# Stores of folded attention weights moved behind the first spreads of B, dt and C, with one fold kept in the scan's tiles

## The chip, the cores and the metric

The kernel runs on one core of a Trainium2 chip. The metric is the device time of one execution in microseconds (us), the median of three runs. A profile was taken of one further execution; its times count from the start of its span. TensorE, VectorE, ScalarE and GpSimd stand in the profile as PE, DVE, ACT and POOL, the queue from which most transfers are issued as SP. A "q" behind an engine's name means its instruction queue.

## The reference, cut to what matters

The input x is an image of 2 x 128 x 64 x 64 (batch, channels, height, width), in float32. Four layers follow each other. Layer 0 is a small Mamba network with two blocks over the 4096 pixels as a sequence; layer 1 is attention over all pixels whose q, k and v come from 3x3 convolutions; layer 2 is the same kind of attention with 1x1 convolutions; layer 3 fuses four scales. The change lies in layer 0 and in the preparation of layer 1's convolution weights:

```python
dbl = u @ xproj_w.T
dt, Bm, Cm = jnp.split(dbl, [R, R + N], axis=-1)
dt = jax.nn.softplus(dt @ dt_w.T + dt_b)
dA = jnp.exp(dt[..., None] * A)
dBu = (dt * u)[..., None] * Bm[:, :, None, :]

def step(h, inp):
    dA_t, dBu_t, C_t = inp
    h = dA_t * h + dBu_t
    y = jnp.einsum('bdn,bn->bd', h, C_t)
```

Here the inner width is 256, there are 16 states per channel, and u is the activated result of a short convolution. In layer 1:

```python
q = conv2d(x, Wq, bq, 1).reshape(b, c, n)
k = conv2d(x, Wk, bk, 1).reshape(b, c, n)
v = conv2d(x, Wv, bv, 1).reshape(b, c, n)
```

## The kernel before, in words

**Items, groups and slots.** Layer 0 is cut into 32 items: 2 images, 2 blocks, 8 pieces of 512 tokens. Each item has 8 groups of 32 channels. A group's tile h is 128 x 4 x 512: its partitions are 4 sets of states by 32 channels, and 4 states per set lie behind one another. So a group takes one product on VectorE that makes dBu (`times_b`, L389), four decays on ScalarE that make dA (`decay`, L396), four scans on VectorE (`scan`, L407), the product with C on GpSimd (L410), and matmuls that sum over the states (`y_pair`, L422).

A slot is one scan; an item has 32 slots, numbered 0 to 31, and a group has four. The order of all instructions is written out by hand: for every item i and every slot the function `slot` issues the group's own work, and then what `background(i)` has put on that slot's list with `at(slot, function, ...)`. Each engine, and the SP queue, takes its instructions in this order. The background of item i prepares item i + 1 and finishes items i - 1 and i - 2. Items -2 and -1 have no scans; their slots prepare item 0.

**What scans need.** The small projection of an item is in the tile dbl (`xproj_out`, L343, slot 14). `spread_bc` stores its B and C part to a DRAM tile dr (L349, only with B) and loads it back four times with a broadcast over 32 partitions each (L354): B into the tile bb in slot 14, C into the tile cb in slot 22. `spread_dt` copies a group's 32 rows of dt four times, into the four quarters of the tile dtb (L378); `slot` calls it for group g + 3 at the beginning of group g, so the dt of group 0 stands in slot 20 of item -1, that of group 1 in slot 24, of group 2 in slot 28, and of group 3 in slot 0 of item 0. The first product of item 0 stands in slot 26 of item -1, its first decay in slot 28, its first scan in slot 0 of item 0.

**The folds.** Layer 1's 3x3 convolutions are computed from weights combined beforehand. In item -1, `load_rest` (slot 1) issues the loads of three raw weight tiles and of the second image. `fold(k)` for k = 0, 1, 2 (slots 8, 9, 10) makes two tiles ulo and uhi of 128 x 9 x 128 from raw k with ten VectorE instructions (L195 to L204), and stores each to a DRAM tile ufold (L206). They are loaded again (L604, L858) after the scans, about 2096 us into the span.

**Buffers.** The raw weights, the folds' results, the convolution weights cw, the scan's h and the hidden tile of the feed-forward part share one ring of five buffers, tag "h". bb and cb have two buffers each. A new tile takes the buffer that was released first, and its first writer waits for the last user of that buffer. Eight semaphores serve the transfers in turn.

Of the kernel before, what the change touches and what calls it, by code (L numbers as in the profile page):

```python
# [6 lines left out]
F32 = mybir.dt.float32  # L7
# [6 lines left out]
B, C, H, W = 2, 128, 64, 64  # L14
N = H * W
P = 128
# [51 lines left out]
def tile_conv_seq(ctx: ExitStack, tc, x, consts, vecs, wemb, wlay, wconv, wdt, wqkv, wsmall, wms, out):  # L68
# [47 lines left out]
    with tc.manual_schedule(), ExitStack() as s:  # L116
# [4 lines left out]
        sp = scans.enter_context(tc.tile_pool(name="l0s", bufs=1, side="right"))  # L121
# [48 lines left out]
                nc.vector.tensor_tensor(u[:, k, :], cw[:, KC, :], cw[:, k, :], ALU.mult)  # L170
            wu.append(u), am.append(a)

        raws = []

        def load_rest():
            for which in range(3):
# [13 lines left out]
        def fold(which):  # L190

            g = [raws[which][:, :, k, :] for k in range(3)]
            lo, hi = (sp.tile([P, 3, 3, C], F32, name=n, tag="h", bufs=5) for n in ("ulo", "uhi"))
            tt, ts, stt = nc.vector.tensor_tensor, nc.vector.tensor_scalar, nc.vector.scalar_tensor_tensor
            tt(lo[:, 1], g[0], g[2], ALU.add)  # L195
            ts(lo[:, 1], lo[:, 1], -1.0 / 6, None, ALU.mult)
            stt(lo[:, 0], g[1], 1.0 / 6, lo[:, 1], ALU.mult, ALU.add)
            stt(lo[:, 1], g[1], -1.0 / 6, lo[:, 1], ALU.mult, ALU.add)
            stt(hi[:, 0], g[2], 4.0, g[0], ALU.mult, ALU.add)
            ts(hi[:, 0], hi[:, 0], 1.0 / 24, None, ALU.mult)  # L200
            stt(lo[:, 2], g[1], -1.0 / 12, hi[:, 0], ALU.mult, ALU.add)
            stt(hi[:, 0], g[1], 1.0 / 12, hi[:, 0], ALU.mult, ALU.add)
            ts(hi[:, 1], g[0], 0.25, None, ALU.mult)
            nc.vector.tensor_copy(hi[:, 2], g[2])  # L204
            for k, u in enumerate((lo, hi)):
                nc.sync.dma_start(ufold[which][:, 9 * k : 9 * k + 9, :], u.rearrange("p s y c -> p (s y) c"))  # L206


# [9 lines left out]
        def has(i):  # L218
            return 0 <= i < NI
# [269 lines left out]
        def background(i):  # L489

            todo = [[] for _ in range(NSL)]

            def at(t, f, *a):
                todo[t].append((f, a))

            n, p, q, r = i + 1, i - 1, i - 2, i + 2
            if has(q):
                at(3, gelu, q)
                at(6, ffn_down, q, (0, 1)), at(7, ffn_down, q, (2, 3)), at(9, ffn_add, q)
                at(11, out_mm, q), at(12, out_add, q)  # L500
            if has(p):
                at(7, y_out, p, 1), at(7, gate, p)
                at(9, mix_out, p), at(11, mix_add, p)
            if has(n):
                at(0, pu_taps, n, 0, (0, 1)), at(1, pu_taps, n, 0, (2, 3)), at(2, pu_out, n, 0)
                at(3, pu_taps, n, 1, (0, 1)), at(4, pu_taps, n, 1, (2, 3)), at(5, pu_out, n, 1)
                at(13, xproj, n), at(14, xproj_out, n), at(14, spread_bc, n, 0), at(22, spread_bc, n, 1)
                at(15, dtproj, n, 0), at(16, dtproj, n, 1), at(17, soft_plus, n), at(18, dt_end, n)
            if has(i):
                at(1, pz_mm, i, 0), at(3, pz_out, i, 0)  # L510
                at(5, pz_mm, i, 1), at(6, pz_out, i, 1)
            if has(i) or has(n):
                at(11, silu, i, n)
            if i == -1:
                at(1, load_rest), at(7, prepare, 1)
                for k in range(3):
                    at(8 + k, fold, k)
                at(19, spread_dtu, 0), at(26, times_b, 0)
            pair = [(k, second) for k, second in ((p, True), (r, False)) if has(k)]
            if has(r):  # L520
                at(10, embed, r), at(11, embed_out, r)
            w, m = {}, len(pair)
            for k, (it, second) in enumerate(pair):
                at(12 + 2 * k, ln_centre, w, k, it)
                at(13 + 2 * k, ln_square, w, k, it)
                at(27, ln_spread, w, k, m), at(28, ln_scale, w, k, it)
                at(29, ln_shift, w, k, it, second)
            if pair:
                at(17, ln_var, w, m), at(18, ln_eps, w, m), at(19, ln_rs, w, m), at(20, ln_newton, w, m), at(21, ln_step, w, m)
            if has(p):  # L530
                for f in range(4):
                    at(30 + f // 2, ffn_up, p, f)
            if has(i):
                at(24, y_out, i, 0)
            return todo
# [23 lines left out]
        for i in range(-2, NI):  # L559
            todo = background(i)  # L560
            for t_ in range(NSL):
                slot(i, todo, t_)
        todo = background(NI)
        for t_ in range(8):
            slot(NI, todo, t_)
# [321 lines left out]
        for k in range(8, 2 * NSL):  # L887
            if k == NSL:
                todo = background(NI + 1)
            for _ in range(int(beside[k - 8]) if k - 8 < len(beside) else 0):  # L890
                next(steps, None)
            slot(NI + k // NSL, todo, k % NSL)
# [4 lines left out]
        sp = s.enter_context(tc.tile_pool(name="ats", bufs=1, reuse_waits="tile"))  # L897
        psa = s.enter_context(tc.tile_pool(name="atpa", bufs=2, reuse_waits="tile", space=PSUM))
        psm = s.enter_context(tc.tile_pool(name="atpm", bufs=1, reuse_waits="tile", space=PSUM))
        for now in range(NALL + LAG + 10):  # L900
            r, u = divmod(now, NU)
# [71 lines left out]
    with ExitStack() as s, tc.manual_schedule():  # L973
        sp = s.enter_context(tc.tile_pool(name="mss", bufs=1, reuse_waits="tile"))
# [494 lines left out]
```

## Time and profile before

| what | value |
|---|---|
| median of three runs | 5001.07 us (5000.54 to 5005.86) |
| the profiled execution, its time | 5004.69 us |
| the profiled execution, its span | 5002.9 us |
| PE busy | 4661.3 us, 93% of the span |
| DVE busy | 4024.6 us, 80% |
| ACT busy | 2358.8 us, 47% |
| POOL busy | 2337.5 us, 47% |
| scans (L407), 1024 of them | 1241.6 us, 1.27 us each |
| products with B (L389), 256 of them | 581.7 us, 2.27 us each |
| decays (L396), 1024 of them | 681.5 us, 0.68 us each |

The scans of layer 0 run from 73 to some 2090 us, the two attentions and layer 3 follow. A row of the timeline has the start in us, the duration in us, the engine, the line of the kernel, the operation, the tile written and the tiles read, the shapes, how many such instructions were merged, and in brackets how long the engine was idle before and what ended that. For SP the duration of a row is the time in which its transfers were issued, not the time that they took. In a DMA view the stretch is cut into 40 equal parts; one line gives the busy share of the 16 DMA engines in tenths, another the rate in GB/s.

### The profile page before, as it was taken

How to read it: one execution, taken by the hardware profiler on the slowest of the kernel's cores; microseconds unless marked ns; L12 is line 12 of the kernel's file. 1: busy time of each engine (PE TensorE's matmuls, PEld its weight loads, DVE VectorE, ACT ScalarE, POOL GpSimd, SP SyncE). 2: the span in 40 equal slices, each digit the busy share in tenths (PEclk: the TensorE clock that was granted, in tenths of full speed). 3: DMA queues.
4: the chain of work that ended last, by engine and by line, in shares of the span. 5: the costliest groups of instructions: out<-in, count | busy, mean ns of one | idle time of the engine just before them, and what ended most of it. 6: DMA issues, size and time to landing. Idle time of an engine off the chain costs nothing. (4 is left out here: it accounts for less than half of the span.)

```text
span 5002.9 us, 48954 instructions
## 1 busy us (share of the span) xinstructions
PE 4661.3 (93%) x14797; PEld 2242.4 (45%) x14797; DVE 4024.6 (80%) x4283; ACT 2358.8 (47%) x3218; POOL 2337.5 (47%) x1974
## 2 busy tenths in 40 slices
PE   5889999999988899899999999999999999999997
PEld 1222222222222222366667766666666666333332
DVE  6999999999999999878886677767776775667776
ACT  4677777777777777522222222233333332323332
POOL 3777776766777777513332133333333332333331
PEclk8898889989999989899999999999999999999998
DMA  6333333322323333214444344434443443000000
GB/s 163 69 68 68 69 71 70 69 65 62 72 67 68 70 73 73 73 53 113 109 110 123 105 112 111 120 95 114 110 100 98 112 113 88 3 7 7 5 7 9
DMA packets 242343, 386.24 MB, mean 77 GB/s; under 512 B 88592, under 2 KB 88992, under 8 KB 233632
## 3 DMA queue, kind: packets, MB, share of 16 engines
q1 hardware_dynamic: 192928, 315.94, 26.0%
q10 hardware_dynamic: 49152, 67.17, 5.4%
q8 instruction: 118, 1.93, 0.2%
q14 instruction: 145, 1.19, 0.1%
HBM read 101.02 MB, written 13.37 MB: 23 GB/s over the span
## 5 line engine op out<-in xcount | busy, mean ns | idle before, releaser
L792 POOL COPY pt<-tr 32x512 f32<-32x512 f32 x1024 | 650.8, 636 | 1437.3 <-DVE tr L785 704.7
L407 DVE TENSOR_TENSOR_SCAN h<-da,carry,h 128x512 f32<-128x512 f32 x1024 | 1241.6, 1266 | 59.7 <-ACT da L396 30.7
L410 POOL TENSOR_TENSOR h<-h,cb 128x2048 f32<-128x2048 f32 x256 | 1160.9, 4535 | 21.0 <-POOL carry L409 0.4
L755 PE MATMUL pq<-k,q 128*128 128x512 f32 x2048 | 962.6, 593 | 7.0 <-DVE sc L760 7.0
L805 PE MATMUL po<-pt,vt 128*128 128x256 f32 x4096 | 965.7, 379 | 2.5 <-DMA pt<-tr 2.5
L770 ACT ACTIVATE sc<-sc,nm 128x2048 f32<-128x2048 f32 x256 | 510.6, 1995 | 912.8 <-DVE nm L766 701.6
L805 PEld LDWEIGHTS po<-pt,vt 128*128 128x128 f32 x4096 | 777.9, 190 | 294.8 <-issue 208.3
L760 DVE TENSOR_SCALAR_CACHE_REDUCE sc<-pq 128x1024 f32<-128x1024 f32 x512 | 625.1, 1222 | 315.6 <-PE pq L755 294.3
L396 ACT ACTIVATE da<-dtb,am 128x512 f32<-128x512 f32 x1024 | 681.5, 684 | 230.5 <-DVE h L407 207.9
L389 DVE TENSOR_TENSOR h<-bb,pdu 128x2048 f32<-128x2048 f32 x256 | 581.7, 2272 | 86.0 <-PE py L422 29.3
L785 DVE STREAM_TRANSPOSE tr<-sc 128x2048 f32<-128x2048 f32 x256 | 591.6, 2311 | 64.6 <-DMA pt<-tr 56.2
L422 PE MATMUL py<-h,sel 128*32 128x512 f32 x2048 | 511.0, 643 | 1.6 <-POOL h L410 1.6
L755 PEld LDWEIGHTS pq<-k,q 128*128 128x128 f32 x2048 | 382.9, 190 | 283.2 <-issue 247.2
L383 PE MATMUL pdu<-dtu,fsel 128*128 128x512 f32 x512 | 325.3, 721 | 117.0 <-DVE h L389 114.8
L422 PEld LDWEIGHTS py<-h,sel 128*32 128x32 f32 x2048 | 115.2, 117 | 415.0 <-issue 409.5
L310 PE MATMUL pu<-xn,wu 128*128 128x512 f32 x512 | 246.2, 614 | 2.6 <-ACT xn L300 1.7
L383 PEld LDWEIGHTS pdu<-dtu,fsel 128*128 128x128 f32 x512 | 95.9, 214 | 322.0 <-DVE h L389 199.5
L409 POOL COPY carry<-h 128x4 f32<-128x4 f32 x256 | 47.8, 187 | 394.5 <-DVE h L407 392.7
L1219 DVE TENSOR_TENSOR ov<-v,pw 128x2048 f32<-128x2048 f32 x64 | 146.2, 2285 | 62.1 <-PE pw L1212 62.1
L1153 PE MATMUL pqkv<-f,ws 128*128 128x512 f32 x384 | 188.2, 615 | 3.0 <-DVE prod L1170 2.3
L1223 POOL TENSOR_TENSOR ov<-ov 128x2048 f32<-128x2048 f32 x16 | 72.6, 4538 | 235.5 <-DVE ov L1219 235.5
L370 POOL TENSOR_TENSOR dtu<-dt,u 128x1024 f32<-128x1024 f32 x32 | 75.1, 2348 | 192.6 <-ACT dt L364 192.6
(259 smaller groups left out, 5266.6 us busy)
## 6 DMA issues: line engine op xcount, KB each, us to landing
pt<-tr SPq DMA_DIRECT2D x2048, 64.0 KB, 2.0
dtb<-dt SPq DMA_DIRECT2D x1024, 64.0 KB, 2.0
pt<-tr ACTq DMA_DIRECT2D x1024, 64.0 KB, 2.2
bb<-dr SPq DMA_DIRECT2D x128, 256.0 KB, 4.4
cb<-dr SPq DMA_DIRECT2D x128, 256.0 KB, 4.6
uw<-ufold SPq DMA_DIRECT2D x12, 576.0 KB, 4.3
uw<-dkept SPq DMA_DIRECT2D x20, 288.0 KB, 3.0
xt<-in_x SPq DMA_DIRECT2D x16, 256.0 KB, 4.6
```

The costliest lines, as they stand in the source:

```text
L383: nc.tensor.matmul(pdu, lhsT=four(s_ % 4), rhs=st[i]["dtu"][:, s_ // 4, :], start=True, stop=True)
L389: nc.vector.tensor_tensor(h, st[i]["bc", 0], pdu.unsqueeze(1).to_broadcast([P, 4, CH]), ALU.mult)
L396: nc.scalar.activation(da, st[i]["dtb", s_], AF.Exp, scale=am[items[i][1]][:, j, gg, m : m + 1])
L407: nc.vector.tensor_tensor_scan(h[:, m, :], da, h[:, m, :], carries[b, l][:, j, gg, m : m + 1], ALU.mult, ALU.add)
L410: nc.gpsimd.tensor_tensor(h, h, st[i]["bc", 1], ALU.mult)
L422: nc.tensor.matmul(py[r : r + 32, :], lhsT=sel, rhs=st[i]["h", s_ + k][:, m, :], start=(m == 0), stop=(m == 3), tile_position=(0, r),)
L755: nc.tensor.matmul(pq[:, i, :], lhsT=sta["q", r, grp][:, it * P : (it + 1) * P], rhs=sta["k"][:, at : at + CH], start=True, stop=True)
L760: nc.vector.tensor_scalar(dst, pq, 1.0, None, ALU.mult, ALU.max, accum_out=sta["mx"][:, c2 : c2 + 1])
L770: nc.scalar.activation(sc, sc, AF.Exp, bias=nm, scale=scale, accum_out=sm[:, hh : hh + 1])
L785: nc.vector.transpose(tr, sta.pop(("sc", r, blk, hh)).rearrange("p (t r f) -> p r t f", r=NB, f=32))
L792: nc.gpsimd.tensor_copy(dst, src)
L805: nc.tensor.matmul(sta["po", r, grp], lhsT=sta["vt"][:, jt, :], rhs=rhs, start=(jt == 0), stop=(jt == N // P - 1))
```

## The change

The two stores of a fold leave `fold` for a function `fold_out`, and all six stand in slot 23 of item -1, between the spread of C (slot 22) and that of dt of group 1 (slot 24). The results of a fold are kept until then, so more tiles are held at a time. The fold of weight 1 therefore takes its two tiles not from the ring "h" but from the scan's tags "bb" and "cb".

```diff
-        raws = []
+        raws, folded = [], []
...
         def fold(which):
 
             g = [raws[which][:, :, k, :] for k in range(3)]
-            lo, hi = (sp.tile([P, 3, 3, C], F32, name=n, tag="h", bufs=5) for n in ("ulo", "uhi"))
+            tags = (("h", 5), ("h", 5)) if which != 1 else (("bb", 2), ("cb", 2))
+            lo, hi = (sp.tile([P, 3, 3, C], F32, name=n, tag=t, bufs=k) for n, (t, k) in zip(("ulo", "uhi"), tags))
+            folded.append((lo, hi))
...
             nc.vector.tensor_copy(hi[:, 2], g[2])
-            for k, u in enumerate((lo, hi)):
+
+        def fold_out(which):
+            for k, u in enumerate(folded[which]):
                 nc.sync.dma_start(ufold[which][:, 9 * k : 9 * k + 9, :], u.rearrange("p s y c -> p (s y) c"))
...
                 for k in range(3):
-                    at(8 + k, fold, k)
+                    at(8 + k, fold, k), at(23, fold_out, k)
                 at(19, spread_dtu, 0), at(26, times_b, 0)
```

## Prediction

> **What bounds the kernel now.** I read the page first. The chain that ended last is followed only through the attention stages, so it says nothing of the first 100 us, where the change lies. From the windows by stage: from 80 to 2000 us VectorE is busy 394 of 420 us, then 467, 463 and 467 of each 500, and the waits there close a loop: ScalarE's decays wait for VectorE's scans (207.9 us in all) and the scans for the decays (30.7 us). Nothing in that loop hangs on the clock on the wall: the x loads have been issued by 34.5 us. So a scan loop that starts earlier should end earlier by as much, and so should what follows.
>
> What sets the loop's start is in the timeline of the first 130 us (start, duration, engine and line, what ended the idle time before):
>
> ```profile
> 47.32 0.58 ACT L343 COPY dbl<-pd 40x512 f32<-40x512 f32 x1 [2.49 <-PE pd L339]
> ...
> 50.74 2.34 POOL L370 TENSOR_TENSOR dtu<-dt,u 128x1024 f32<-128x1024 f32 x1 [29.36 <-ACT dt L364]
> 51.03 2.47 DVE L195 TENSOR_TENSOR ulo<-raw 128x384 f32<-128x384 f32 x1
> ...
> 58.72 0.32 SPq L206 DMA_DIRECT2D ufold<-ulo  x1
> ...
> 59.67 0.54 DVE L204 COPY uhi<-raw 128x384 f32<-128x384 f32 x1
> 60.24 0.32 SPq L206 DMA_DIRECT2D ufold<-uhi  x1
> 60.65 0.40 SPq L349 DMA_DIRECT2D dr<-dbl  x1
> 63.30 1.71 SPq L354 DMA_DIRECT2D bb<-dr  x4
> 65.11 2.50 SPq L378 DMA_DIRECT2D dtb<-dt  x4
> 67.66 3.07 SPq L354 DMA_DIRECT2D cb<-dr  x4
> 70.49 2.29 DVE L389 TENSOR_TENSOR h<-bb,pdu 128x2048 f32<-128x2048 f32 x1 [10.28 <-DMA bb<-dr]
> ...
> 77.48 1.91 ACT L396 ACTIVATE da<-dtb,am 128x512 f32<-128x512 f32 x3 [2.10 <-DMA dtb<-dt]
> ...
> 80.44 4.81 DVE L407 TENSOR_TENSOR_SCAN h<-da,carry,h 128x512 f32<-128x512 f32 x4
> ```
>
> The small projection dbl is ready at 47.90, but its store dr leaves only at 60.65: SP stands on the six fold stores, the last of which waits for VectorE's last fold copy (60.21). Then comes the train dr, B, dt, C, and VectorE is idle for 10.28 us until B has landed. The second stall to keep in mind is at 77.48: ScalarE waited for the second group's dt, behind C in the queue.
>
> The DMA view tells what the transfers cost. From 44 to 53 us, the first four fold stores; from 62.5 to 78 us, the train:
>
> ```profile
> GB/s 0 0 0 0 0 143 389 410 369 471 389 430 226 410 369 471 410 410 348 0 0 0 0 0 0 0 0 0 225 410 369 451 430 389 348 287 369 471 389 430
> ```
> ```profile
> DMA  6000967997978997889998989979989869999425
> ```
>
> A fold store (576 KB, 0.59 MB) moves at about 400 GB/s, 1.47 us of all engines, and lands 2.8 us after issue. The train keeps the DMA engines full from 64 to 76.5 us at some 210 GB/s; its landings come in the order of issue, a 256 KB spread each 1.27 us, then a group's four dt pieces at 0.26 us each. Before the change the stores filled a DMA that was otherwise idle; that cover goes.
>
> **What the Trainium skill says.** "DMA: Bandwidth & Descriptors", "Queues, rings and completion order": on each DMA engine a queue's descriptors are consumed in ring order. The trace agrees (landings in order of issue). It means that a transfer issued behind the stores is behind their bytes too. The same page, "Bandwidth", gives some 358 GB/s as a core's share of HBM; the single stores here reach about 400, and six in a row are not shown, so both serve as ends. "SBUF — State Buffer", "SBUF: two separate sides": VectorE with two SBUF inputs and GpSimd take turns on a shared port, held for a whole instruction. The trace agrees: the fold at 51.03 took 2.47 us, not its usual 0.55, while GpSimd's product ran from 50.74 to 53.08; two more took 1.61 and 1.66. So the folds end at 60.21 because of GpSimd, not because of stores, and the change leaves that as it is.
>
> **The change part by part.**
> *The stores leave the head of the queue.* dr issues at 47.95 instead of 60.65: 12.70 us earlier. It then lands in 1.6 us (the second item's dr, on an idle queue) and not 2.65 (60.65 to 63.30, behind a store). B's spreads issue at 49.55: 13.75 earlier. dt is ready at 50.65 (49.21 + 1.44), before its spreads' turn at 51.4, so the train moves whole: B landed at about 56.7 (was 70.4), dt of group 0 at 57.7, C at 62.6 (was 76.3).
> *VectorE.* Its instructions and their order are the same; the folds still end at 60.21. B is no longer last: the first product starts at 60.25, not 70.49, a gain of 10.24. Then the stall is VectorE's own queue. cen follows, the first scan starts at 63.1 (was 73.35), and the second product ends near 70.1.
> *The stores come back ahead of dt of group 1.* They stand in slot 23, the second group's dt in slot 24. SP issues them from about 57 to 60.6; a transfer also waits for the landing of the eighth before it (seen at 69.17 and 70.42, where the third and fourth C pieces left as the third and fourth B landed), which holds back dt's pieces to about 65.5, no further than the data itself. Their 3.54 MB move behind C's: 3.54 MB / 400 GB/s = 8.8 us, to 62.6 + 8.8 = 71.4. dt of group 1 lands last, plus 1.05 (four pieces): about 72.4. A decay takes 0.68 and starts 0.11 after the landing, and the scan 0.06 after it: the second group's scan starts at 73.25. VectorE alone would be there at 80.44 − 10.24 = 70.20, so 3.05 us of the gain go back. Net: 80.44 − 73.25 = **7.2 us**. Dt of groups 2 and 3 lands by 74 and 76, needed from 80 on.
> *The ends of that.* With no delay by the stores the gain is 10.2. With 358 GB/s, 3.54 MB take 9.9 us: gain 6.1. At the spreads' 210 GB/s, 16.9 us: loss of 0.9 against before. I take 400, because each store alone shows it.
> *Tiles.* The fold of which = 1 takes the first bb and cb buffers; B and C of item 0 get the second ones, unused, so no wait. B of item 1 needs the first back: its turn is near 99 (106.54 before, less 7), the store lands by 69. In ring h, the order of release gives the first product raw2's buffer (freed by VectorE's own fold) and the second the first fold's ulo, whose store lands at about 64.1 and is needed at 67.8: hidden by 3.7 us; were it later, the stall at 73.25 would hide 3 us more. The waits of folds on earlier folds' stores vanish, worth nothing (they had passed). SP, ScalarE, TensorE and GpSimd gain no instruction.
> *ScalarE's queue.* Its wait for dt of group 1 holds the next item's pu_out back (80.24 to about 74.4, a gain of 5.8, not 7.2); the next item's B is needed only at 130, so this is covered by tens of us.
> *The end of the scans.* Because bb and cb are first used earlier, they lie ahead of dbl and dt in SBUF, and the attention's weight tile comes to lie on dt, dtu and dtb, no more on cb. Its loads waited until 2096.43 for GpSimd's last product and landed by 2103.2, used from 2104.76; now they can leave some 4.5 us earlier. That use waited for VectorE (uw L622), not for the load, so this is worth nothing.
>
> Sum: −7.2 us. On the profiled execution: 5004.69 − 7.2 = 4997.5. That execution lies 3.6 us above the median of 5001.07, so on the median: **4993.9 us**.
>
> **Rivals.**
> *The stores hide.* If they overlap C's slow spreads (210 of 400 GB/s used), dt of group 1 is there by 69.4 and the whole 10.2 us stay: 4990.8 us. For it: that spare rate. Against: the DMA engines read as full during the spreads.
> *The gain mostly goes back.* Stores at 250 to 358 GB/s, or a later wait in the loop that swallows part: gain 0 to 6, 4995 to 5001 us. For it: stores and spreads have not been seen mixed. Against: every later wait is within the loop.
> *The stores stop the scan.* One mechanism, at dt of group 1: it breaks even when that lands at 79.6 (80.44 less 0.85), that is with the stores at 222 GB/s from 62.6 on. At the spreads' 210 it is 5002 us. Slower by 0.2% needs a landing at 89.6, a rate near 136 GB/s: 5011 us. For it: HBM traffic both ways at once is not shown. Against: 400 GB/s in every store.
> *Nothing changes* would need the loop not to be bound by its start; the 10.28 us of idle VectorE speak against it.
>
> **How the numbers follow.** Runs of before span 5000.5 to 5005.9, so about 0.2%, 10 us, is what can be told from no change. Chances: 7.2 us gain as worked out (6 to 9), 0.58; the whole 10.2, 0.2; mostly given back, 0.18; stopped, 0.04. The first lies within 0.2%, with a tail of 0.07 beyond by scatter; the second, right at the limit of 4991.1, gives 0.13 to faster. So faster 0.2, same 0.76, slower 0.04. The range of 4988 to 5001 takes in the whole gain with scatter below, and the gain given back above.
>
> **What would show it.** dr at 48, B at 49.6, the first product at 60.25 directly behind the last fold copy, six stores between 57 and 60.6, dt of group 1 landing at 72.4, and a VectorE wait of about 3 us for da before the scan at 73.25; from then on each product 7 us earlier than before, through to the first attention product at 2097.6. The prediction is wrong if dt of group 1 lands by 69.5 or after 75, if the first product waits for a store, or if the shift shrinks between 80 and 2100 us.

## The result, and the profile after

| | before | after |
|---|---|---|
| median of 12 runs each, alternating | 5005.83 us (5000.20 to 5007.83) | 4996.24 us (4989.93 to 5001.15) |
| ratio, with its 95% interval | | 0.9983 [0.9975, 0.9991] |
| profiled execution, its span | 5002.9 us | 4994.0 us |

The medians differ by 9.6 us; the ratio says 8.5 us, between 4.5 and 12.5. In the two profiles shown, the spans differ by 8.9 us. In the changed kernel the lines below the edit lie four further down: dr is stored at L353, B and C are spread at L358, the folds are stored at L210, the product with B is L393, the decay L400, the scan L411.

The same stretch of the timeline as in the prediction, of the changed kernel (start, duration, engine and line, operation, tiles, count, and in brackets the idle time before and what ended it):

```profile
45.29 0.58 ACT L347 COPY dbl<-pd 40x512 f32<-40x512 f32 x1 [2.49 <-PE pd L343]
45.90 0.34 SPq L353 DMA_DIRECT2D dr<-dbl  x1
47.53 1.72 SPq L358 DMA_DIRECT2D bb<-dr  x4
...
55.00 0.37 SPq L210 DMA_DIRECT2D ufold<-ulo  x1
...
57.72 0.54 DVE L206 COPY uhi<-raw 128x384 f32<-128x384 f32 x1
...
58.35 2.29 DVE L393 TENSOR_TENSOR h<-bb,pdu 128x2048 f32<-128x2048 f32 x1
59.33 24.24 SPq L382 DMA_DIRECT2D dtb<-dt  x24
...
69.89 1.91 ACT L400 ACTIVATE da<-dtb,am 128x512 f32<-128x512 f32 x3 [6.65 <-DMA dtb<-dt]
70.62 4.81 DVE L411 TENSOR_TENSOR_SCAN h<-da,carry,h 128x512 f32<-128x512 f32 x4 [2.43 <-ACT da L400]
71.75 0.67 ACT L320 ACTIVATE u<-pu,vec 128x512 f32<-128x512 f32 x1
72.47 3.32 PE L314 MATMUL pu<-xn,wu 128*128 128x512 f32 x4 [3.66 <-ACT u L320]
...
75.57 1.43 PE L387 MATMUL pdu<-dtu,fsel 128*128 128x512 f32 x2
...
77.04 2.29 DVE L393 TENSOR_TENSOR h<-bb,pdu 128x2048 f32<-128x2048 f32 x1 [1.62 <-PE pdu L387]
```

dr now leaves 0.03 us after dbl is ready (45.87), not 12.7 us later. The first product at 58.35 stands directly behind the last fold copy, and has no bracket: the 10.28 us of idle time are gone. Two new waits follow. The scan of the second group waits 2.43 us for a decay, which waited for dt behind the stores. The third product then waits 1.62 us for TensorE. In the kernel before, the decay of this group waited too, 2.10 us on ScalarE, but neither the scan (80.44) nor the third product had to wait on VectorE:

```profile
85.16 2.26 DVE L389 TENSOR_TENSOR h<-bb,pdu 128x2048 f32<-128x2048 f32 x1
```

The DMA view of the changed kernel from 56 to 74 us, in 40 parts of 0.45 us (busy share of the engines in tenths, then the rate):

```profile
DMA  9999998789899999999999999999975365246336
GB/s 200 219 200 255 200 237 166 174 307 461 369 451 420 430 430 389 461 369 461 420 420 430 389 451 379 451 367 383 269 160 109 64 146 123 59 109 141 77 73 146
```

The spreads of C run at some 200 GB/s up to 59.6 us, the six stores at some 420 after it, to 68.6. They do not mix. The stores landed at 61.67, 63.05, 64.43, 65.81, 67.2 and 68.61 us, 1.39 apart in the mean (576 KB / 1.39 us = 424 GB/s); dt of group 1 landed behind them, at 69.79.

**The parts of the 8.9 us.** Every kernel here can be cut at two events: the end of dbl, and the start of the last of the 256 products with B near 2075 us. Between them lies what the change can move; ahead of it lie the loads, the folds and the preparation of item 0, behind it the attentions and layer 3.

| part of the span, us | before | after | difference |
|---|---|---|---|
| start to dbl | 47.90 | 45.87 | −2.03 |
| dbl to last product with B | 2035.82 | 2028.87 | −6.95 |
| last product with B to the end | 2919.19 | 2919.22 | +0.03 |

So the change is worth 6.95 us in this pair. The other 2 us come ahead of dbl, and the experiments must say whose they are.

### The profile page after: what moved, and what is told of

Its sections match the earlier page's. It is cut to its first block, busy times and chain, and to the rows that moved or that the text cites. A ratio compares the mean times of both kernels' runs of the same rounds, so it can differ in the third digit from the quotient of the medians.

```text
span 4994.0 us, 48951 instructions
## 1 busy us (share of the span) xinstructions
PE 4661.7 (93%) x14797; PEld 2242.2 (45%) x14797; DVE 4022.4 (81%) x4283; ACT 2358.4 (47%) x3218; POOL 2335.3 (47%) x1974
## 4 chain that ended last, share of the span: by engine, by line
PE 46%; POOL 24%; issue 12%; DVE 9%; DMA 3%; SPq 2%; ACT 2%; ACTq 0%; DVEq 0%; POOLq 0%
POOL h L414 19%; PE po L809 13%; PE pq L759 13%; DVE tr L789 3%; DMA pt<-tr 3%; PE pa L656 2%; PE pf L1130 2%; SPq L800 2%; PE pqkv L1157 2%; PE pw L1216 1%; POOL dtu L374 1%; POOL z L437 1%; PE pb L656 1%; PE pfus L1281 1%; PE psc L1181 1%
## 5 line engine op out<-in xcount | busy, mean ns | idle before, releaser
L411 DVE TENSOR_TENSOR_SCAN h<-da,carry,h 128x512 f32<-128x512 f32 x1024 | 1240.7, 1265 | 62.0 <-ACT da L400 31.8
L400 ACT ACTIVATE da<-dtb,am 128x512 f32<-128x512 f32 x1024 | 681.4, 684 | 220.9 <-DVE h L411 207.6
L393 DVE TENSOR_TENSOR h<-bb,pdu 128x2048 f32<-128x2048 f32 x256 | 581.3, 2271 | 77.6 <-PE py L426 29.4
L413 POOL COPY carry<-h 128x4 f32<-128x4 f32 x256 | 47.7, 186 | 389.8 <-DVE h L411 389.8
```

The source lines that it names most:

```text
L393: nc.vector.tensor_tensor(h, st[i]["bc", 0], pdu.unsqueeze(1).to_broadcast([P, 4, CH]), ALU.mult)
L400: nc.scalar.activation(da, st[i]["dtb", s_], AF.Exp, scale=am[items[i][1]][:, j, gg, m : m + 1])
L411: nc.vector.tensor_tensor_scan(h[:, m, :], da, h[:, m, :], carries[b, l][:, j, gg, m : m + 1], ALU.mult, ALU.add)
```

## The experiments

The theory is that of the prediction: the gain is VectorE's 10.2 us of idle time, less what the stores' bytes cost the dt of group 1 behind them. Its rivals: the stores hide and the tiles or the start do the rest; the layout matters; the stores' issue and not their bytes costs time. Below, "+" times are counted from the end of dbl in the same execution, so that most of the start drops out.

**The two kernels again.** Both unedited, each beside others on one chip.

> The kernel before once more, beside the changed one. If the start varies by itself, dbl is ready anywhere from 45.5 to 48.5 us, and from dbl to the first product it is 22.6 us as in the first profile, to the third product 37.3 us. If the earlier start belongs to the change, dbl is again at 47.9. Time 5001 to 5006 us.

> The changed kernel once more. My theory splits the 8.9 us between the two profiles into the moved stores (6 to 7 us) and a difference in the start that has nothing to do with the change: dbl was ready 2.0 us earlier in the profile after, because TensorE's first convolution (pu, 16 matmuls) took 8.8 and not 9.9 us. If so, dbl's time (45.9 after, 47.9 before) varies between executions of either kernel, while the stretch from dbl to the second group's scans stays: first product 12.5 us after dbl, second group's scan 24.7 us after it, third product 31.1 us after it. Rival: the earlier start belongs to the change; then dbl stays at 45.9 here and at 47.9 for the kernel before.

> The kernel before, for the start alone. In ten profiles TensorE's matmuls of the first pu begin within 24.9 to 25.2 us, and their spacing drops from 0.98 to 0.43 us somewhere between 28.5 and 31.1; dbl follows, 44.9 to 47.9. The two profiles of the kernel before lie at the late end. If the moment of the drop is by chance, it lies anywhere in that range here; if it belonged to the change, this kernel would be late again, 30.1 or more, dbl 47.5 or more, each time.

> As the run before it; one of the two before 30 us would show that the start belongs to no kernel. From dbl to the third product again 36.8 to 37.3 us.

> The changed kernel once more, for its time beside the next and for the start: from dbl to the second group's scan 24.3 to 24.8 us, to the last product with B 2029 us after dbl; 0.9985 of the kernel before.

| run | dbl | last fold ends | first product | first scan of group 1 | third product | last product | its rest to the end |
|---|---|---|---|---|---|---|---|
| before | 47.90 | +12.31 | +22.59 | +32.54 | +37.26 | +2035.82 | 2919.19 |
| before_again | 47.49 | +12.30 | +22.16 | +32.10 | +36.83 | +2035.41 | 2915.72 |
| before_3 | 47.65 | +12.30 | +22.66 | +32.61 | +37.34 | +2035.67 | 2915.75 |
| before_4 | 45.99 | +12.53 | +22.77 | +32.71 | +37.44 | +2035.78 | 2915.82 |
| after | 45.87 | +12.39 | +12.48 | +24.74 | +31.17 | +2028.87 | 2919.22 |
| after_again | 45.92 | +12.39 | +12.48 | +24.33 | +30.69 | +2029.00 | 2922.51 |
| after_3 | 47.70 | +12.30 | +12.40 | +24.65 | +31.08 | +2028.72 | 2919.23 |

From dbl to the last product, before takes 2035.41 to 2035.82 and after 2028.72 to 2029.00: means of 2035.67 and 2028.86, so the change is worth 6.8 us, with a scatter of some 0.4. The start belongs to neither kernel: before_4 has dbl at 45.99, and after_3 has it at 47.70. What differs is TensorE's pace. Two rows of the timeline of before, then the same two of the changed kernel:

```profile
25.15 9.88 PE L310 MATMUL pu<-xn,wu 128*128 128x512 f32 x16 [1.68 <-ACT xn L300]
...
38.82 2.04 PE L235 MATMUL pe<-xt,we 128*128 128x512 f32 x2
```

```profile
25.12 8.83 PE L314 MATMUL pu<-xn,wu 128*128 128x512 f32 x16 [1.68 <-ACT xn L304]
...
37.74 1.10 PE L239 MATMUL pe<-xt,we 128*128 128x512 f32 x2 [0.30 <-PE pa L163]
```

The first rows begin within 0.03 us of each other. Their first matmuls start 0.85 us apart (the very first pair 0.98), the later ones 0.43. In before the change of pace falls at 31.00, after seven at the longer spacing, in after at 28.64, after four; the granted clock, TensorE's share of its full speed, goes from half to full at 30.74 and 28.60. Over all fourteen profiles it falls anywhere from 28.48 to 31.05, after four to seven of them, on either kernel. This makes the first rows end 1.1 us apart (35.03 and 33.95). The other 0.9 us come from the second rows: near 38 us the granted clock falls to half again, at 37.57 in before, ahead of its two matmuls, and at 38.84 in the changed kernel, behind them. So the 2 us are twice the same thing. The Trainium skill, "TensorE: Matmul & The Clock Gate", section "What's actually happening", says that TensorE runs at half rate until a free-running window of 3.4 us has been busy, so that the moment depends on where the window stands when the first matmul comes. The profiles agree with such a lottery, though their spread of 2.6 us is wider than the 0.5 us either way which that section gives; it fits better with the section's note that the number of slow matmuls varies from run to run.

In times, beside before at 5004.07 us, before_again had 5004.52, ratio 1.0001 [0.9993, 1.0009], and after_again 4995.90, ratio 0.9985 [0.9979, 0.9992]. Beside 5005.06 for before, after_3 had 4996.17, ratio 0.9983 [0.9975, 0.9990]; before_3 and before_4 were one execution each, 5000.86 and 4999.41. The gain of the medians, 7.5 to 8.5 us by these ratios, is within its scatter of the 6.8.

**The tiles alone.** Before, with the fold of weight 1 in bb and cb, the stores unmoved:

```diff
-            lo, hi = (sp.tile([P, 3, 3, C], F32, name=n, tag="h", bufs=5) for n in ("ulo", "uhi"))
+            tags = (("h", 5), ("h", 5)) if which != 1 else (("bb", 2), ("cb", 2))
+            lo, hi = (sp.tile([P, 3, 3, C], F32, name=n, tag=t, bufs=k) for n, (t, k) in zip(("ulo", "uhi"), tags))
```

> The kernel before with one part of the change alone: the fold of weight 1 in the tags bb and cb, the stores where they were. My theory: the tiles do nothing by themselves, neither the places of tiles in SBUF that move with them nor the waits at the end of the scans; same as the kernel before within 0.1%, first product 22.6 us after dbl, 37.3 us from dbl to the third product. Rival: some of the gain comes from the new places (the attention's weights no longer wait for GpSimd's last product with C); then this one is 1 to 4 us faster than before, and the gain is seen behind 2090 us.

First product at +22.20, first scan of group 1 at +32.14, last product at +2035.59: all as before. The time is 5000.73, ratio 0.9994 [0.9986, 1.0003], which takes in no change. So neither the tiles nor the layout of memory that follows from them does anything that is seen here.

**The stores six slots later.** The changed kernel, with the stores behind the dt of groups 1 and 2:

```diff
-                    at(8 + k, fold, k), at(23, fold_out, k)
+                    at(8 + k, fold, k), at(29, fold_out, k)
```

> The changed kernel with the six stores in slot 29 instead of 23: behind dt of groups 1 and 2. My theory: the second group's scan waits in the changed kernel because its dt stands behind the stores' bytes in the same rings, and the third product waits because ScalarE and TensorE were held up with it. Both waits (2.4 and 1.6 us) go, the second group's scan starts 22.4 us after dbl and not 24.7, the third product 27.2 and not 31.1; 4 us faster than the changed kernel, about 0.9975 of the kernel before. Rival: something else bounds the third product (TensorE's own work at the low clock); then the first wait goes and the third product still comes 29 us or more after dbl, and the gain over the changed kernel is under 2.5 us. Third: the second product now waits for the first store (its buffer); then it starts later than 20.1 us after dbl.

> The stores in slot 29 once more: from dbl to the second group's scan 22.3 us, to the last product with B 2025.7 us after dbl; 3 us faster than the changed kernel on the median, about 0.9979 of the kernel before.

The timeline of stores_29, same columns:

```profile
56.91 6.13 SPq L382 DMA_DIRECT2D dtb<-dt  x8
...
63.14 0.53 SPq L210 DMA_DIRECT2D ufold<-ulo  x1
...
70.28 4.81 DVE L411 TENSOR_TENSOR_SCAN h<-da,carry,h 128x512 f32<-128x512 f32 x4
...
75.01 2.26 DVE L393 TENSOR_TENSOR h<-bb,pdu 128x2048 f32<-128x2048 f32 x1
```

Eight dt transfers now leave ahead of the first store, and neither the scan of the second group nor the third product has a bracket. dbl ended at 47.94 here, so the scan of group 1 stands at +22.34 (with the stores in slot 23: +24.57 in the mean), the third product at +27.06 (+30.98), the last product at +2025.67, and +2025.49 in the repeat. That is a gain of 10.1 us, the whole idle time. The medians are 4992.79, ratio 0.9978 [0.9969, 0.9987], and 4993.69, ratio 0.9977 [0.9969, 0.9985]. So both new waits of the changed kernel come from the stores' place in the queue, and that place costs 3.3 us (10.1 − 6.8). This is read from the profiles, two of which agree here within 0.2 us; the intervals of the medians overlap that of the changed kernel.

**The next item's projection two slots later.** This takes TensorE's matmuls for pu, which stand ahead of those of the third product, out of its way:

```diff
-                at(3, pu_taps, n, 1, (0, 1)), at(4, pu_taps, n, 1, (2, 3)), at(5, pu_out, n, 1)
+                a = (3, 4, 5) if i != 0 else (5, 6, 7)
+                at(a[0], pu_taps, n, 1, (0, 1)), at(a[1], pu_taps, n, 1, (2, 3)), at(a[2], pu_out, n, 1)
```

> The changed kernel with one thing moved: in item 0 the second half of the next item's convolution (pu, slots 3 to 5) goes to slots 5 to 7, so that on TensorE the spread of the third group's dtu (pdu, slot 4) stands ahead of it. My theory: the third product waits 1.6 us in the changed kernel because pdu stands behind pu, pu behind ScalarE's pu_out, and that behind the decays that wait for dt. Then the first wait stays (second group's scan 24.3 to 24.7 us after dbl) and the second goes: third product 29.1 to 29.4 us after dbl, not 30.7 to 31.2. Rival: pdu is late by itself, at TensorE's low clock or behind VectorE's second product; then the third product stays at 30.5 us or more.

```profile
70.91 4.81 DVE L411 TENSOR_TENSOR_SCAN h<-da,carry,h 128x512 f32<-128x512 f32 x4 [2.34 <-ACT da L400]
...
75.63 2.26 DVE L393 TENSOR_TENSOR h<-bb,pdu 128x2048 f32<-128x2048 f32 x1
...
95.25 2.63 DVE L411 TENSOR_TENSOR_SCAN h<-da,carry,h 128x512 f32<-128x512 f32 x2 [0.61 <-ACT da L400]
```

In this timeline of pu_later the first wait is there with 2.34 us, and the second is gone: the third product, at +29.41, has no bracket. That settles where the 1.62 us come from. ScalarE stands on the decay that waits for dt, so the activation behind it in its queue (u, L320, at 71.75 in the changed kernel) is late, TensorE's four matmuls for pu wait for that, and the third product's own two wait behind those. But the 1.8 us by which pu_later leads the changed kernel at the third product (+29.41 against +31.17) are 0.7 at the sixth (+52.08 against +52.78) and nothing at the last (+2029.16 against +2028.87). Part of it goes at 95.25, where a scan waits 0.61 us for a decay; ScalarE, which takes that decay in its turn, had stood 3.51 us on the next item's preparation, waiting for TensorE. Where the rest goes was not followed. The median is 4997.31, ratio 0.9984 [0.9978, 0.9991]. Moving pu is worth nothing.

**The stores from ScalarE's queue.** The changed kernel, with the stores in the same slot but on another queue:

```diff
-                nc.sync.dma_start(ufold[which][:, 9 * k : 9 * k + 9, :], ...)
+                nc.scalar.dma_start(ufold[which][:, 9 * k : 9 * k + 9, :], ...)
```

> The changed kernel with the six stores issued from ScalarE's queue instead of SP's, in the same slot 23. My theory: dt of group 1 is late because it stands in the same rings behind the stores. In another queue's rings the stores share the engines with it, and dt lands some 17 us after dbl, not 24: second group's scan about 22.4 us after dbl, third product 27.2, nearly as with the stores in slot 29. ScalarE's first decay waits for the last fold, about 13 us after dbl and not 10, which the first scan at 15.3 covers. Rival: the engines work through all transfers in the order in which they were issued, whatever the queue; then the second group's scan stays at 24.3 or later.

Neither reading was borne out. The timeline of act_queue:

```profile
47.55 11.38 SPq L358 DMA_DIRECT2D bb<-dr  x4
...
54.78 0.38 ACTq L210 DMA_DIRECT2D ufold<-uhi  x1
...
64.88 2.29 DVE L393 TENSOR_TENSOR h<-bb,pdu 128x2048 f32<-128x2048 f32 x1 [6.63 <-issue]
```

SP needs 11.38 us for the four spreads of B, which took 1.72 in the changed kernel: its fourth leaves only at 58.63, 0.02 us after the second store on ScalarE's queue has landed (58.61). In the records of the trace both name the same semaphore: the eight that serve the transfers in turn are handed out over both queues, the second store had this one, and the spread waits on it. B landed at 64.70, so VectorE was idle for 6.63 us before the first product (+19.03; its bracket gives "issue" for want of a better match), and the last product is at +2032.00: 3.7 us of gain are left. The median is 4999.59, ratio 0.9987 [0.9979, 0.9996]. Whether stores on a queue of their own would hold up the dt behind them can't be read from this run, since the new wait comes first; it stays open.

**Each store twice.** The changed kernel, with every store issued a second time, to a spare tensor in DRAM that nothing reads; that traffic is no part of the reference:

```diff
                 nc.sync.dma_start(ufold[which][:, 9 * k : 9 * k + 9, :], ...)
+                nc.sync.dma_start(uspare[which][:, 9 * k : 9 * k + 9, :], ...)
```

> The changed kernel with each of the six stores issued a second time to a spare tensor: 7.1 MB in place of 3.54 ahead of dt of group 1. If a store costs 1.38 us of the rings, as the landings of the changed kernel show, dt of group 1 lands 8.3 us later, about 32.3 us after dbl, and the second group's scan starts at 33.0, past the 32.1 to 32.5 of the kernel before: the gain is gone, 5003 to 5006 us. The rival that the wait is something other than bytes (issue, semaphores) expects 2 to 3 us more for six further issues: scan at 26.5 to 27.5.

The timeline of stores_twice, in which the decay is L402 and the scan L413:

```profile
77.33 1.91 ACT L402 ACTIVATE da<-dtb,am 128x512 f32<-128x512 f32 x3 [13.21 <-DMA dtb<-dt]
78.06 4.81 DVE L413 TENSOR_TENSOR_SCAN h<-da,carry,h 128x512 f32<-128x512 f32 x4 [8.98 <-ACT da L402]
```

The twelve stores landed 1.41 us apart, dt of group 1 at +32.3, and the scan began at +33.17 (dbl: 44.89): twice the bytes, 8.6 us more than with six. The last dt piece of group 1 left at 70.44, held by the semaphores, but landed only 6.7 us later (6.7 in the changed kernel too, from 63.06 to 69.79), where a later dt piece, with no store ahead, took 2.0 there: it is the bytes that bind, not the issue. (With dbl so early the folds end only at +14.26 and the first product stands at +14.35; the scan waits for its dt all the same.) The last product is at +2037.29, 1.6 us later than before. The median is 5008.15, above what was expected, beside 5005.67 for before: ratio 1.0007 [0.9999, 1.0016], which takes in no change. The rival in which the stores stop the scan has its law right: the whole gain is gone when dt of group 1 lands at about the time that the prediction named for it (79.6, which is +31.7).

**The first fold in an earlier gap.** The changed kernel, with the stores in slot 29, the fold of weight 0 in slot 5 and in the scan's tiles in place of weight 1:

```diff
-            tags = (("h", 5), ("h", 5)) if which != 1 else (("bb", 2), ("cb", 2))
+            tags = (("h", 5), ("h", 5)) if which != 0 else (("bb", 2), ("cb", 2))
...
-                for k in range(3):
-                    at(8 + k, fold, k), at(23, fold_out, k)
+                at(5, fold, 0), at(8, fold, 1), at(9, fold, 2)
+                for k in (1, 2, 0):
+                    at(29, fold_out, k)
```

> The stores in slot 29, and the fold of weight 0 in slot 5, ahead of the second block's preparation, where VectorE is idle; it takes the bb and cb buffers instead of the fold of weight 1. With the stores in slot 29 the first product waits for nothing but VectorE's own folds (12.4 us after dbl; B lands at 8.7). With one fold earlier they end by 5 us after dbl. My theory: the first product starts at 8.8, but the next VectorE instruction, cen, waits for TensorE's pr until 12.5, so the first scan starts at 13.2 instead of 15.2 and the third product at 25.0 instead of 27.1: 2 us faster than with slot 29 alone. Rival: the early fold delays the block's preparation on VectorE, and dbl with it; then dbl comes 1 to 5 us later and nothing is gained.

The timeline of early_fold:

```profile
54.81 2.29 DVE L393 TENSOR_TENSOR h<-bb,pdu 128x2048 f32<-128x2048 f32 x1 [5.05 <-DMA bb<-dr]
...
58.21 0.75 DVE L291 SCALAR_TENSOR_TENSOR cen<-cen,vec,pr 128x512 f32<-128x512 f32 x1 [1.11 <-PE pr L287]
...
64.23 2.29 DVE L393 TENSOR_TENSOR h<-bb,pdu 128x2048 f32<-128x2048 f32 x1 [0.55 <-DMA ufold<-ulo]
```

The folds now end at +3.98, and B is last again: the first product waits 5.05 us for it and starts at +9.04, 3.4 us earlier than in the changed kernel. Two new waits take some of that back: 1.11 us for TensorE before the next item's centring, and 0.55 us of the second product for a store that still holds its tile. The third product is at +25.58, 1.5 us ahead of stores_29, the last one at +2025.18, only 0.4 ahead. The median is the lowest of all, 4990.52, ratio 0.9972 [0.9961, 0.9983], and faster than before; the interval overlaps those of stores_29 and of the changed kernel, so that it is the profile (10.5 against 6.8 in the table below) that sets it ahead of the latter.

| run | gain from dbl to the last product, us | ratio of the medians |
|---|---|---|
| changed kernel | 6.8 | 0.9983 to 0.9985 |
| tiles_only | 0.1 | 0.9994 |
| stores_29, twice | 10.0 and 10.2 | 0.9978, 0.9977 |
| pu_later | 6.5 | 0.9984 |
| act_queue | 3.7 | 0.9987 |
| stores_twice | −1.6 | 1.0007 |
| early_fold | 10.5 | 0.9972 |

Each gain is 2035.67, the mean of the four profiles of before, less the run's own +time. They stand in the order of the ratios, as far as these can tell them apart.

## Why the prediction was right

The time of 4996.24 us lies 2.3 above the forecast of 4993.9 and within its range, and the mechanism is the one forecast. That the level agrees so well is in part luck: the forecast took 7.2 from a median of three, 5001.07, and the median of twelve for before is 5005.83, so that the medians now differ by 9.6. By its steps, with its times counted from dbl at 47.90:

- *dr leaves at once, B follows 1.6 us later.* As worked out: 0.03 us after dbl, and B's spreads 1.63 after dr.
- *The first product directly behind the last fold.* Forecast +12.35, measured +12.48, +12.48 and +12.40. The bound was indeed to become VectorE's own queue; stores_29 keeps the whole 10.1 us to the end of the scans, against the 10.2 worked out.
- *The stores' bytes hold dt of group 1.* The rate taken was 400 GB/s, so 1.47 us a store; measured 1.39. dt was to land at +24.5 and landed at +23.9; the stall was to be 3.05 us and was 2.43. The mechanism was right, and this term too large by 0.6. That it is bytes is shown by stores_twice, where the scan moves by 8.6 us for 3.54 MB more.
- *ScalarE's queue, "covered by tens of us".* This step failed. It followed the held activation only to the next item's B. It is TensorE that needs it sooner: its queue has the next item's pu matmuls ahead of the third product's, and that product waited 1.62 us.
- *What of that remains.* The place of the stores costs 3.3 us by the last product. From the means, the changed kernel leads before by 7.9 us at the scan of group 1, where 7.2 was forecast, and by 6.2 at the third product, behind the wait of 1.62 for TensorE that the forecast had not. Later 0.6 come back, and 6.8 remain. So that 6.8 is near 7.2 is luck in part: the stall was forecast too large, and a wait was missed. What this wait alone is worth is open: pu_later, which is without it, leads by 7.8 at the third product but by 7.2 at the sixth and 6.5 at the last.
- *Once in the loop, the shift stays.* At its ends only: after leads before by 6.2 us at the third product, 6.5 at the sixth and 6.8 at the last. In between it is not constant. At the 65th product the three profiles lead the mean of before by 8.8, 8.7 and 7.0 us, and at the last by 6.8, 6.7 and 7.0; why two of them gain and lose 2 us on the way is not shown. The first attention product, at 2104.76 in before, comes at 2095.78, 9.0 us earlier, of which 2.0 are the start.
- *Tiles and handover to the attention worth nothing.* tiles_only shows it for the tiles. The rest after the last product is 2919.19 and 2919.22 in the first pair, but in the means of all profiles of the two kernels it is 3.7 us longer with the change, so that their spans differ by only 3.9. The last section shows where this comes from. It may be chance: only three of the fourteen profiles have the short rest of 2915.7 to 2915.8, all of them of before. The medians speak against a loss of that size, since 6.8 − 3.7 = 3.1 us lies outside all three intervals of the changed kernel, whose lower ends are 4.0 to 5.0 us.

Of the rivals, "the stores hide" falls: they come after C and not beside it. "Mostly goes back" falls with a gain of 6.8. The sizes of the medians' differences (7.5 to 9.6 us) are not evidence for more than 6.8, nor the mean spans for less; a single pair of profiles would have given 8.9, and so credited the change with 2 us of the start.

## What to carry to other kernels

A wait at the head of an in-order queue is best followed with the whole train behind it: here it was VectorE's slow last fold that kept a small store, and so the scans, waiting, and moving six transfers behind that train freed 10 us. Where they are put back decides how much of it stays: bulk stores cost their bytes to whatever is next in the same queue, so they belong behind the last transfer that someone will soon wait for (3.3 us here for six slots). And a wait is charged to every queue that stands behind the waiting instruction, not to the next consumer of its data alone; still, a wait that is seen (1.62 us) is no promise of a gain, as pu_later showed.

## What the runs showed of the hardware

- Six stores of 576 KB from SBUF back to back land 1.39 us apart, 424 GB/s, twelve 1.41 us apart. The prediction had kept 358 GB/s as its lower end, from the Trainium skill, "DMA: Bandwidth & Descriptors", section "Bandwidth". The part "Where 436 GB/s comes from" of the same section gives 435 as the ceiling of the engines' ports, and says that for transfers with HBM the 358 bind; here the measured rate is just below the first, and the second, which the section's note on its table puts at both cores of a pair streaming, did not bind on a core that ran alone.
- TensorE's change from 0.85 to 0.43 us a matmul came from 3.5 to 6 us after its first projection matmul, on either kernel, over fourteen profiles. Together with a fall back to the slower pace near 38 us it moved dbl, and everything behind it, by up to 3 us (44.89 to 47.94).
- The rest of the program after the last product with B took 2915.7 to 2915.8, 2919.2 to 2919.5, 2922.5 or 2925.9 us, so in steps of about 3.4, on kernels whose work there is the same. The granted clock shows where one such step arises. This is the stretch from 3235 to 3310 us in before, then in before_again (busy time of PE, PEld, DVE, ACT and POOL in us with the instructions in brackets, then the share of the full TensorE clock that was granted, the busy share of the DMA engines, and GB/s):

```profile
3235.00:3310.00 75.00, 69.08 (x240) 43.46 (x241) 43.74 (x64) 23.53 (x33) 17.74 (x29) 0.95 0.42 114
3235.00:3310.00 75.00, 70.15 (x254) 44.77 (x255) 44.97 (x66) 23.64 (x33) 17.13 (x28) 1.00 0.41 111
```

In before the clock is at half twice here, for 3.41 us each, in before_again never. Counted from the last product, VectorE's instructions in before are 0.2 us behind those of before_again ahead of the first such stretch, 1.8 behind it and 3.5 after the second, and so to the end. So the step here is two stretches of half rate at some 1.6 us each. In all, TensorE stood at half rate in the rest for 60.3 to 60.4 us in the three shortest profiles, 63.6 to 63.8 in eight of the nine of the next step (67.2 in the ninth, act_queue), and 67.1 and 73.9 in the two longest. Why it falls to half in one execution and not in another is not shown.
- The transfer semaphores, which serve in turn, tie two queues together: in act_queue a spread on SP's queue waited 9.8 us for a store on ScalarE's.
